# Score steps over four row groups, values begun with the later heads, and a new written order in a two-layer attention and expert kernel

## Chip, core and metric

The kernel runs on one NeuronCore of one Trainium2 chip. The metric is the device time of one execution in microseconds (us). Three runs of the kernel before gave 589.65, 581.01 and 583.12 us; their median is 583.12.

## What is computed

The input is 4 sequences of 512 tokens of width 128, in float32. Two layers follow each other, each of the form x + attention(norm(x)) * silu(experts(norm(x))).

```python
x = L0_attn_x                                   # (4, 512, 128)
xn = _layernorm(x)
s = _L0_attn_ref(xn, ...)                       # 16 heads of 8: compressed + selected + windowed
g = _silu(_L0_ffn_ref(xn, ...))                 # 8 experts, the best 2 of each token
x = x + s * g
xn = _layernorm(x)
s = _L1_attn_ref(xn, ...)                       # 16 heads of 8, full softmax attention, own norm
g = _silu(_L1_ffn_ref(xn, ...))                 # 8 experts, one result kept for each token
x = x + s * g
```

Layer 0's attention adds three softmax attentions weighted by a gate: over 32 compressed blocks of 16 tokens, over the first 8 tokens of the two best blocks, and over a window of 32 tokens. Layer 1's attention is dense over 512 keys.

## The kernel before

The four sequences are called b = 0 to 3. PE is TensorE, DVE VectorE, ACT ScalarE, POOL GpSimd, SP the queue that starts most transfers.

**Layer 0 attention** (`attn0`, L720). Heads lie in four groups of four; a group of four heads is 32 rows of q and k, so one group is one row group of the PE array (`g32`, rows 32g to 32g+31). Windowed scores: for each parity `e` of the 16 blocks of 32 keys and each pair `k` of groups, one step writes 8 blocks x 2 groups of matmuls (L739, 32 rows x 128 columns of weights, 64 columns streamed; each float32 matmul appears as two instructions) into one pair of PSUM banks (`pair`, tag "s", two such pairs exist). The next step is the Exp on ACT (L748), the next the mask product on DVE (L751). Compressed scores (L756, Exp L766, mask L768) go the same way, a pair of groups at a time; selected scores (L780) use two row groups of 64. Then for each half of the tokens two steps of output matmuls (L819, L827, L835) and one step of normalising on DVE (L845 to L866) follow, then transposes, the projection (L880) and its sum.

**Experts** (`experts`, L314). Tokens are sorted by expert through a dispatch (L191) that computes, for tiles of 128 rows, which rows to fetch (`where`, L311) and whose weights to load. Layer 0 has 46 tiles in two dispatches, layer 1 has 23. Four coroutines serve them: `weights` (a 578 KB load from SP, four buffers, L328), `fetches` (an indirect gather from POOL, L339), `hidden` (transposes L354 once for four tiles, their copy L357, then eight matmuls L362 and the relu, L374 on ACT in layer 0 and L376 on DVE in layer 1), and `outputs` (eight matmuls L387, the bias sum L396 on DVE, an indirect scatter from POOL, L399).

**Layer 1 attention** (`attn1`, L1048). There are 64 units: b, four groups `t` of four heads, four blocks `k` of 128 keys. `scores` has three steps for a unit: four matmuls (L1065, one for each head, each in its own row group, two PSUM pairs of tag "s", hp = 0 and 1), then the Exp of hp 0, then that of hp 1 (L1074, 128 x 1024 each). `values` has one step for a unit: eight instructions of L1085 (four heads, each in its own column group of 32, twice for float32) that add into one PSUM bank over four units, and after the fourth a copy out by DVE (L1095). `turned` transposes (L1103), divides (L1109, L1110) and projects (L880).

**The order.** Nothing is scheduled by the compiler: every strand of work is a coroutine named by a character, and `ORDER` (L60) is a string in which each character runs the next step of its strand. Every engine then takes its instructions strictly in that order, and each transfer stands in its queue where it was written. The characters: 0 to 3 norms and logits, 4 to 7 the entry into layer 1, 8 and 9 set-up, a and b the two dispatches of layer 0, c to f values, g to j keys, k to n layer 0's attention, o, p, q, r its weights, fetches, hidden and outputs, s buffers, t and u layer 1's router, v its dispatch, w scores, x values, y to B the turned parts, C, D, E, F layer 1's weights, fetches, hidden and outputs, G to K the end. In layer 1 the old string often reads `wwFwEFECFw`: scores, Exp, an expert's output matmuls, Exp, hidden matmuls of a later tile, the bias sum, its relu, a weight load, a scatter, the next scores.

Written out from that string, with ST for a unit's score matmuls and AV for its values, the old order has units 21 to 24 as: ST22, Exp, AV21, Exp, AV22, ST23, Exp, y of tile 1, Exp, hid of tile 3, ST24.

Of the kernel before, what the change touches and what calls it, by code (L numbers as in the profile page):

```python
# [12 lines left out]
F32 = mybir.dt.float32  # L13
# [3 lines left out]
AF = mybir.ActivationFunctionType  # L17
# [3 lines left out]
P = 128  # L21
B, S, D = 4, 512, 128
# [7 lines left out]
QB = 32  # L30
NJ = S // QB
# [4 lines left out]
SCALE = float(1.0 / np.sqrt(HD))  # L36
# [21 lines left out]


ORDER = """  # L60
v88290282920232032100301301g31g31g3cg1ccg1agggaacggkkaggkkkkkkkkkaakkgkggkkkgaahokpokhohpkaaohap
kpccppcdddkabpphdkhhkqkpqhpqphhkpqhhrkqqkhqkqkhbrklrrlobhqqqhrlolrqrblpqqdpdpidrpleolbrereilqrlo
qrlrlqrelqrlrlqrlqrlrlqrllrqrlpbbbpipllprirlbbbbilliloooiloliqleqlielriqqrmeorrmqrmoqrrqrqorrqrm
pqoiiqmirqrpqprqmomrirmpqrmoqrrqqroqrrqpqrqorrqprqomrrmpqrmoqrrqprqoqrrqpqrqorrqpqromrrmqprqmomr
rmpqrqmoqrrqpqroqrrqprq4mrorm5pqrmoqrrqprqoqrrq4qrqorr44q5qr4oirfp4rfp5fqrqio4j5r4rjpjr5oqrfqrjp
qrm4q4j54mjrjpm4pqqpjrpq4rjjrm5qr55jjrqoq5omjor5rjsqrqfofrrfmq4pq5ppppppppr4oqq4r5rttqtqjqqrmtrr
jmttqrqrrqmrqrrmnrrnnnnonnnonnnonnno44nnnq4q4rnnrrqnqnnrnrrqnqrnrronssoooooqnqr4nrrqnq5n5q5nqwwr
wqrrqqwrw4wrrr4xwwxwxww6wx7wxwy5w5y6x575ww67wx676www6x76ww66wx7wxw6y6wxy7w77w6w76x75ww6w76w67wxu
wxuuww5wwwxv5wxvwwxwxuuuwvwywvxywxwvvwxCCDwCwyDCywxyD6Dww6Dwy6xD6yDwwEyDwxDEyEDxEwDwzEzDwExwwFwE
FEFwwxCwxwwFwE6FECFwwE6DwxE6DwxDw7wzD7x7zwwxwxwwFwEFEFwwxwFxEFEFwwzxzwCwCwxwxwwF7wEFECFwwxw7xw7w  # L70
z7xzwzwwzxzwwwzwxzwwxwFxwFwEFEwExDECwDwxDwxD7ww7wA7xAwxwFwEFECFwwxwxwwFwEFECFwwxwxwxwFwEFECFwwxw
xwwFwEFECFwwExDwEwDwxDDDDDDDDwFEFECFwwFwEFECFAFxAEFECFxwwxwxwwFwEFECFEwEFwEwFECFFEFECFFxFCFEEwwF
wEFECFEFEEFECCCCCFFAFExFEFAxFFEEEwwAxAwAwwxwxwxwAFAwxFFwwAwFAwFwBFFxBwwwBxBwGwwxwxwwBwxBGwGGwxHH
wxGGIIwGGwGwwJJxxxBBBBBBBKK
"""


# [19 lines left out]
class Kernel:  # L97
# [622 lines left out]
    def attn0(self, b, got, gates, pool):  # L720

        nc = self.nc
        a = got[b]
        qT = a["qT"]
        pair = lambda n: self.psum.tile([P, 2, 512], F32, tag="s", name=f"{n}_{b}", bufs=2)
        split = lambda t: t.rearrange("p (k s) -> p k s", s=S)
        pw, pc = [], []
        g32 = lambda g: slice(32 * g, 32 * g + 32)
# [2 lines left out]
        wm = bc(self.cst[:, T_WM : T_WM + 2 * QB], 1, NJ)  # L731
        for e in range(2):
            pw.append(split(self.shared("kx", 2, 4 * S, f"pw{e}_{b}")))
            for k in range(2):
                ps = pair(f"sw{e}{k}")
                for jj in range(NJ // 2):
                    j = 2 * jj + e
                    for g in (2 * k, 2 * k + 1):
                        nc.tensor.matmul(  # L739
                            ps[:, g % 2, jj * 2 * QB : (jj + 1) * 2 * QB],  # L740
                            a["kw"][g32(g), j].rearrange("p h r -> p (h r)"),
                            qT[g32(g), j * QB : (j + 2) * QB],
                            start=True,
                            stop=True,
                        )
                yield
                t = pw[e][:, 2 * k : 2 * k + 2, :]
                nc.scalar.activation(t, ps, AF.Exp, scale=SCALE)  # L748
                yield
                t = t.rearrange("p g (j q) -> p (g j) q", q=2 * QB)  # L750
                nc.vector.tensor_tensor(t, t, wm, ALU.mult)  # L751
                yield
        for k in range(2):
            ps = pair(f"sc{k}")
            for g in (2 * k, 2 * k + 1):
                nc.tensor.matmul(  # L756
                    ps[:, g % 2, :],
                    a["kc"][g32(g)].rearrange("p h n -> p (h n)"),
                    qT[g32(g), 0:S],
                    start=True,  # L760
                    stop=True,
                )
            yield
            t = split(self.shared("p1", 4, 2 * S, f"pc{k}_{b}"))
            pc.append(t)
            nc.scalar.activation(t, ps, AF.Exp, scale=SCALE)  # L766
            yield
            nc.vector.scalar_tensor_tensor(  # L768
                t,
                bc(self.cst[:, T_QI : T_QI + S], 1, 2),  # L770
                self.vec(V_CP),
                t,
                ALU.is_ge,
                ALU.mult,
            )
            yield
        ps = pair("ss")
        for k in range(2):
            r = slice(64 * k, 64 * k + 64)
# [4 lines left out]
                start=True,  # L784
                stop=True,
# [17 lines left out]
        for half in range(2):  # L803
            ps = pair(f"o{half}")
            for i in range(2):
                t = 2 * half + i
# [4 lines left out]
                for g in range(4):  # L811
                    for prev in range(2):
                        for c in range(4):
                            q = 4 * t + c
# [11 lines left out]
                for g in range(4):  # L826
# [4 lines left out]
                        start=True,  # L831
# [216 lines left out]
    def attn1(self, got, pool):  # L1048
# [6 lines left out]
        def scores():  # L1055
            for u in units:
                b, t, k = u
                qs, ks = got[b]
                ps = []
                for hp in range(2):  # L1060
                    n = f"st_{b}_{t}_{k}_{hp}"
                    ps.append(self.psum.tile([P, 2, 512], F32, tag="s", name=n, bufs=2))
                    for i in range(2):
                        r = slice(32 * (2 * hp + i), 32 * (2 * hp + i) + 32)
                        nc.tensor.matmul(  # L1065
                            ps[hp][:, i, :], ks[r, t, k * P : (k + 1) * P], qs[r, t, :],
                            start=True, stop=True,
                        )
                yield
                p[u] = []  # L1070
                for hp in range(2):
                    e = self.shared("p1", 4, 2 * S, f"p1_{b}_{t}_{k}_{hp}")
                    e = e.rearrange("p (i s) -> p i s", i=2)
                    nc.scalar.activation(e, ps[hp], AF.Exp, scale=SCALE)  # L1074
                    p[u].append(e)
                    yield

        def values():
            for u in units:
                b, t, k = u  # L1080
                va, e = self.va[b % 2], p.pop(u)
                if k == 0:
                    av = self.psum.tile([P, 512], F32, tag="av", name=f"av1_{b}_{t}", bufs=1)
                for h in range(4):
                    nc.tensor.matmul(  # L1085
                        av[32 * h : 32 * h + 32, :],
                        va[:, k, (4 * t + h) * 32 : (4 * t + h) * 32 + 32],
                        e[h // 2][:, h % 2, :],
                        start=(k == 0),
                        stop=(k == NT - 1),  # L1090
                    )
                yield
                if k == NT - 1:
                    o[b, t] = self.shared("vk", 2, S, f"oT_{b}_{t}")
                    nc.vector.tensor_copy(o[b, t], av)  # L1095
                    yield
# [1177 lines left out]
```

## Time and profile before

| | us |
|---|---|
| median of three runs | 583.12 |
| lowest and highest | 581.01 and 589.65 |
| the profiled execution, whole | 598.38 |
| its span, first to last instruction | 596.6 |
| mean granted clock of PE in it | 0.863 of full |
| PE busy in it | 495.1 (83%) |
| VectorE busy | 304.5 (51%) |
| ScalarE busy | 236.6 (40%) |
| first score matmul of layer 1 | 354.3 |
| last values matmuls of layer 1 end | 576.9 |

The costliest rows of the groups, with their busy time: L1074 Exp 124.1 us in 128 instructions; L1085 values 91.2 in 512; L387 and L362, the two expert matmuls, 88.2 and 83.4 in 552 each; L739 windowed scores 38.5 in 512; L1065 scores 38.5 in 256; L756 compressed scores 12.8 in 32.

How to read a profile line: in a group or timeline line, L739 is a line of the kernel, then come the engine, the operation, output <- inputs, shapes and "x" how many instructions. PEld is the weight load of a matmul, which is its own instruction. A bracket gives how long the engine was idle before and who released it. Matmuls are pipelined, so the time from one start to the next says more than a single duration. A line of the table by stages gives, after the stretch and its length, the busy time (and count) of PE, PEld, DVE, ACT and POOL, then PE's granted clock, the share of the transfer engines, and GB/s.

### The profile page before, as it was taken

The numbers are of one execution on the slowest core, as the hardware profiler recorded it, in microseconds if no ns is written. First come the engines' busy times: TensorE is split into PE (matmuls) and PEld (weight loads), VectorE is DVE, ScalarE is ACT, GpSimd is POOL, SyncE is SP. The second block draws the span as 40 slices with busy tenths as digits, with TensorE's granted clock in tenths as the row PEclk, the third lists the DMA queues.
The fourth block names the chain that finished last, engine by engine and source line by source line (L and its number), as shares of the span: only waits on it lengthen the run. The fifth ranks groups of instructions, "written<-read, shape, count | busy, mean of one in ns | idle before, by whom it ended". The sixth has DMA issues, their size and how long they took to land.

```text
span 596.6 us, 11079 instructions
## 1 busy us (share of the span) xinstructions
PE 495.1 (83%) x4203; PEld 341.2 (57%) x4203; DVE 304.5 (51%) x843; ACT 236.6 (40%) x401; POOL 188.3 (32%) x194
## 2 busy tenths in 40 slices
PE   1857788896997989788879988788799999999970
PEld 1646467883876977667766772232354445667420
DVE  1686845955263312376955342868234333246263
ACT  0122103342033245423234235665365766643650
POOL 0300412255004357788520132531623031323100
PEclk9975756798569599997976799998899999999995
DMA  7240540276015367893475345422955643554120
GB/s 215 71 89 1 192 91 19 87 192 203 2 30 162 130 206 235 272 247 96 98 238 196 125 149 153 141 72 73 306 167 149 215 134 101 139 197 163 48 86 24
DMA packets 50160, 82.23 MB, mean 138 GB/s; under 512 B 5505, under 2 KB 30225, under 8 KB 50097
## 3 DMA queue, kind: packets, MB, share of 16 engines
q1 hardware_dynamic: 45104, 71.04, 38.0%
q0 software_dynamic: 4416, 9.05, 6.1%
q10 hardware_dynamic: 576, 1.34, 0.6%
q8 instruction: 35, 0.57, 0.4%
q14 instruction: 29, 0.23, 0.1%
HBM read 64.30 MB, written 17.11 MB: 136 GB/s over the span
## 4 chain that ended last, share of the span: by engine, by line
PE 34%; DVE 10%; issue 6%; ACT 4%; DMA 3%; POOL 1%; SPq 0%; ACTq 0%; DVEq 0%; POOLq 0%
PE av L1085 9%; PE y L387 6%; PE hid L362 5%; PE st L1065 4%; ACT p L1074 3%; PE sw L739 1%; DMA xr<-xs,d_where 1%; PE so L880 1%; PE o L827 1%; PE otr L1103 1%; PE o L819 1%; DMA wt<-in_w 1%; POOL xr L339 1%; PE k L1011 1%; PE sc L756 1%
## 5 line engine op out<-in xcount | busy, mean ns | idle before, releaser
L1074 ACT ACTIVATE p<-st 128x1024 f32<-128x1024 f32 x128 | 124.1, 1024 | 87.5 <-PE st L1065 74.9
L399 POOL DMA_INDIRECT ys<-y,d_where x69 | 77.6, 1125 | 234.4 <-DVE y L396 186.0
L387 PE MATMUL y<-wt,h 128*128 128x128 f32 x552 | 88.2, 307 | 23.4 <-ACT h L374 11.6
L339 POOL DMA_INDIRECT xr<-xs,d_where x69 | 71.3, 1034 | 103.1 <-DVE d_where L311 65.2
L1085 PE MATMUL av<-p,va 128*32 128x512 f32 x512 | 91.2, 619 | 11.1 <-ACT p L1074 9.0
L387 PEld LDWEIGHTS y<-wt,h 128*128 128x128 f32 x552 | 75.7, 208 | 40.1 <-ACT h L374 19.6
L374 ACT ACTIVATE h<-hid,wt 128x128 f32<-128x128 f32 x184 | 52.5, 369 | 101.7 <-issue 56.9
L362 PE MATMUL hid<-xts,wt 128*128 128x128 f32 x552 | 83.4, 299 | 1.8 <-ACT h L374 0.6
L362 PEld LDWEIGHTS hid<-xts,wt 128*128 128x128 f32 x552 | 75.3, 211 | 10.3 <-issue 5.9
L396 DVE TENSOR_TENSOR y<-y,wt 128x128 f32<-128x128 f32 x69 | 20.0, 289 | 113.8 <-PE y L387 92.8
L1085 PEld LDWEIGHTS av<-p,va 128*32 128x32 f32 x512 | 14.2, 109 | 52.4 <-ACT p L1074 40.3
L739 PE MATMUL sw<-qT,kw 32*128 32x64 f32 x512 | 38.5, 330 | 3.3 <-ACT kw L616 3.3
L1065 PEld LDWEIGHTS st<-stq,stk 32*128 32x128 f32 x256 | 15.7, 183 | 43.2 <-issue 25.5
L739 PEld LDWEIGHTS sw<-qT,kw 32*128 32x128 f32 x512 | 36.8, 240 | 4.8 <-ACT kw L616 3.4
L1065 PE MATMUL st<-stq,stk 32*128 32x512 f32 x256 | 38.5, 500 | 1.2 <-ACT p L1074 0.8
L376 DVE TENSOR_SCALAR h<-hid,wt 128x128 f32<-128x128 f32 x92 | 25.9, 345 | 15.5 <-PE hid L362 12.4
L819 PE MATMUL o<-v,pw 128*32 128x36 f32 x992 | 19.9, 225 | 12.2 <-issue 12.1
L748 ACT ACTIVATE pw<-sw 128x1024 f32<-128x1024 f32 x16 | 16.4, 1023 | 31.4 <-PE sw L739 26.1
L819 PEld LDWEIGHTS o<-v,pw 128*32 128x32 f32 x992 | 15.6, 132 | 21.4 <-issue 20.6
L751 DVE TENSOR_TENSOR pw<-pw,c_cst 128x1024 f32<-128x1024 f32 x16 | 19.5, 1222 | 10.1 <-ACT pw L748 9.9
L827 PE MATMUL o<-v,pc 128*128 128x36 f32 x128 | 24.2, 346 | 0.0
L827 PEld LDWEIGHTS o<-v,pc 128*128 128x128 f32 x128 | 22.2, 260 | 1.0
(248 smaller groups left out, 599.7 us busy)
## 6 DMA issues: line engine op xcount, KB each, us to landing
wt<-in_w SPq DMA_DIRECT2D x69, 578.0 KB
v<-drv SPq DMA_DIRECT2D x16, 256.0 KB
drq<-hl SPq DMA_DIRECT2D x16, 256.0 KB
stq<-drq SPq DMA_DIRECT2D x4, 1024.0 KB
drk<-hl SPq DMA_DIRECT2D x16, 256.0 KB
stk<-drk SPq DMA_DIRECT2D x4, 1024.0 KB
yg<-ys SPq DMA_DIRECT2D x12, 256.0 KB
xr<-xs,d_where POOLq DMA_INDIRECT x69
```

The lines of the kernel that those rows point to most:

```text
L339: nc.gpsimd.indirect_dma_start(out=rows[i // 4][:, i % 4, :], out_offset=None, in_=self.xs[ks[i // NS]], in_offset=bass.IndirectOffsetOnAx ...
L362: nc.tensor.matmul(ps[:, f, :], wt[:, W_1 + f * P : W_1 + (f + 1) * P], xt[:, i % 4 * P : (i % 4 + 1) * P], start=True, stop=True,)
L374: nc.scalar.activation(h[:, f, :], ps[:, f, :], AF.Relu, bias=b1)
L376: nc.vector.tensor_scalar(h[:, f, :], ps[:, f, :], b1, 0.0, ALU.add, ALU.max)
L387: nc.tensor.matmul(ps[:, 0:D], g["h"][:, f, :], g["w"][:, W_2 + f * D : W_2 + (f + 1) * D], start=(f == 0), stop=(f == NF - 1),)
L399: nc.gpsimd.indirect_dma_start(out=views[i], out_offset=bass.IndirectOffsetOnAxis(ap=to[:, i % NS : i % NS + 1], axis=0), in_=y, in_offset ...
L739: nc.tensor.matmul(ps[:, g % 2, jj * 2 * QB : (jj + 1) * 2 * QB], a["kw"][g32(g), j].rearrange("p h r -> p (h r)"), qT[g32(g), j * QB : (j ...
L819: nc.tensor.matmul(out(2, g, 4, g32(c)), pw[j % 2][:, g, at : at + QB], flat(a["vw"][:, 4 * j + g]), start=(prev == 0), stop=(prev == 1 or ...
L827: nc.tensor.matmul(out(0, g, 4), pc[g // 2][:, g % 2, t * P : (t + 1) * P], flat(a["vc"][:, g]), start=True, stop=True,)
L1065: nc.tensor.matmul(ps[hp][:, i, :], ks[r, t, k * P : (k + 1) * P], qs[r, t, :], start=True, stop=True,)
L1074: nc.scalar.activation(e, ps[hp], AF.Exp, scale=SCALE)
L1085: nc.tensor.matmul(av[32 * h : 32 * h + 32, :], va[:, k, (4 * t + h) * 32 : (4 * t + h) * 32 + 32], e[h // 2][:, h % 2, :], start=(k == 0) ...
```

## The change

It has four parts.

1. In `attn0` one step now writes the windowed scores of all four row groups, in the order 2, 3, 0, 1, into both PSUM pairs; then come two steps of Exp and two of masks. A b has 28 steps where it had 31.
2. The compressed scores are written likewise: one step of matmuls, two of Exp, two of masks.
3. In `attn1` the score matmuls of hp 1 are written before those of hp 0 (the Exps stay in the order 0, 1), and the four heads of the values are taken in the order 2, 3, 0, 1.
4. `ORDER` is another string, of 1263 characters instead of 1275. In layer 0 its first dispatch stands ahead of batch 0's block choice, the first experts ahead of batch 0's output groups, and batch 1's attention is written together after tile 15 of the experts. In layer 1 each unit's score matmuls are written before the values of the unit ahead of it, in all 63 places; the old order has that in 35 of them and the values first in 28. As an example, units 47 to 49: ST48, transposes of four tiles, Exp, AV47, Exp, y of tile 14, copy of values, ST49, hid of tile 16, Exp, AV48, Exp, y of tile 15.

```diff
 ORDER = """
-v88290282920232032100301301g31g31g3cg1ccg1agggaacggkkaggkkkkkkkkkaakkgkggkkkgaahokpokhohpkaaohap
...
+8v839239232083210301321031021g20gg0cg1ccg1agggacagkgagkgkkkkaaaakkkpgppopokkkkopoggpghpkpqkkqhpq
...
 """
...
         for e in range(2):
             pw.append(split(self.shared("kx", 2, 4 * S, f"pw{e}_{b}")))
+            ps = [pair(f"sw{e}{k}") for k in range(2)]
+            for jj in range(NJ // 2):
+                j = 2 * jj + e
+                for g in (2, 3, 0, 1):
+                    nc.tensor.matmul(
+                        ps[g // 2][:, g % 2, jj * 2 * QB : (jj + 1) * 2 * QB],
+                        a["kw"][g32(g), j].rearrange("p h r -> p (h r)"),
+                        qT[g32(g), j * QB : (j + 2) * QB],
+                        start=True,
+                        stop=True,
+                    )
+            yield
             for k in range(2):
-                ps = pair(f"sw{e}{k}")
-                for jj in range(NJ // 2):
-                    j = 2 * jj + e
-                    for g in (2 * k, 2 * k + 1):
-                        nc.tensor.matmul(
...
+                nc.scalar.activation(pw[e][:, 2 * k : 2 * k + 2, :], ps[k], AF.Exp, scale=SCALE)
                 yield
-                t = pw[e][:, 2 * k : 2 * k + 2, :]
-                nc.scalar.activation(t, ps, AF.Exp, scale=SCALE)
-                yield
-                t = t.rearrange("p g (j q) -> p (g j) q", q=2 * QB)
+            for k in range(2):
+                t = pw[e][:, 2 * k : 2 * k + 2, :].rearrange("p g (j q) -> p (g j) q", q=2 * QB)
                 nc.vector.tensor_tensor(t, t, wm, ALU.mult)
                 yield
+        ps = [pair(f"sc{k}") for k in range(2)]
+        for g in (2, 3, 0, 1):
+            nc.tensor.matmul(
+                ps[g // 2][:, g % 2, :],
...
-                ps = []
-                for hp in range(2):
-                    n = f"st_{b}_{t}_{k}_{hp}"
-                    ps.append(self.psum.tile([P, 2, 512], F32, tag="s", name=n, bufs=2))
+                ps = [
+                    self.psum.tile([P, 2, 512], F32, tag="s", name=f"st_{b}_{t}_{k}_{hp}", bufs=2)
+                    for hp in range(2)
+                ]
+                for hp in (1, 0):
                     for i in range(2):
...
-                for h in range(4):
+
+                for h in (2, 3, 0, 1):
                     nc.tensor.matmul(
```

## Prediction before the changed kernel was run

> **What bounds the kernel now.** I read the page first, then the stages, then TensorE's own timeline in the stages that the change touches. The page (busy row, then tenths of each fortieth of the span):
>
> ```profile
> span 596.6 us, 11079 instructions
> PE 495.1 (83%) x4203; PEld 341.2 (57%) x4203; DVE 304.5 (51%) x843; ACT 236.6 (40%) x401; POOL 188.3 (32%) x194
> PEclk9975756798569599997976799998899999999995
> ```
>
> TensorE (PE) is the only engine near full, and its granted clock is often about half in the first two thirds. The stages (columns: busy us of PE, weight loads, DVE, ACT, POOL, then clock and DMA):
>
> ```profile
> 39.00:96.00 57.00, 46.11 (x418) 34.01 (x419) 39.56 (x104) 11.48 (x16) 13.82 (x12) 0.56 0.28 80
> 96.00:175.00 79.00, 69.47 (x748) 58.98 (x747) 46.70 (x116) 22.78 (x54) 20.09 (x16) 0.74 0.32 91
> 310.00:354.00 44.00, 41.54 (x548) 33.21 (x547) 19.97 (x32) 13.17 (x27) 7.76 (x8) 0.80 0.45 160
> 354.00:432.00 78.00, 63.13 (x379) 25.19 (x378) 43.75 (x132) 42.48 (x52) 28.01 (x30) 0.96 0.49 155
> 432.00:512.00 80.00, 78.11 (x542) 38.48 (x542) 28.06 (x80) 53.29 (x56) 17.03 (x19) 1.00 0.46 150
> ```
>
> PE is 80 to 98% busy in all five; from 432 us on it has no hole. So PE's in-order list sets the time, and the question is what of its "busy" is real work. Layer 1's answer is in its timeline:
>
> ```profile
> 434.28 1.97 PE L1085 MATMUL av<-p,va 128*32 128x512 f32 x8 [0.22 <-ACT p L1074]
> 436.18 0.50 PE L1065 MATMUL st<-stq,stk 32*128 32x512 f32 x4
> 436.61 1.16 PE L387 MATMUL y<-wt,h 128*128 128x128 f32 x8
> 437.60 1.06 PE L362 MATMUL hid<-xts,wt 128*128 128x128 f32 x8
> ...
> 439.20 1.07 PE L1085 MATMUL av<-p,va 128*32 128x512 f32 x8
> ```
>
> The same eight values matmuls take 1.97 us when the second Exp is late (heads 0, 1 run, then 2, 3 a second time through the array) and 1.07, about 0.99 to the next start, when both are there. Over the layer L1085 is busy 91.2 us against 64 units x 1.06 = 67.8: some 23 us are the same array time taken twice.
>
> The scores of layer 0 show the other case. Thirty-two windowed matmuls in two row groups take this, and layer 1's four in four row groups take that:
>
> ```profile
> 123.25 2.00 PE L739 MATMUL sw<-qT,kw 32*128 32x64 f32 x32
> 376.20 0.19 PEld L1065 LDWEIGHTS st<-stq,stk 32*128 32x128 f32 x4 [0.84 <-issue]
> ```
>
> That is 60 ns per matmul (1.93 us to the next start), while one weight load of 32x128 lasts 181 to 187 ns; four loads into four row groups end within 0.19 us, so four go side by side.
>
> [...] here 2.65 us of idle before 74.25 is followed by L827 at 1.7 us for eight, where it takes 0.9 elsewhere[...]. [...]
>
> **The change part by part.**
>
> 1. Windowed scores. Sixteen half-steps become eight steps of four row groups. L739 is busy 12.6 us for b=0, 8.0, 9.7 and 8.2 for b=1 to 3. If four groups cost per step what two do now, half goes. For b=1 to 3, where PE is the bound: 25.9/2 = 12.9 us. For b=0 (39 to 54 us) PE then waits for other work; I count 0. Ends: 0 (no overlap gained), 12.9.
>
> 2. Compressed scores. L756 is busy 12.8 us, 4.1 of it b=0's; half of the other 8.7: 4.3 us. Ends 0 and 4.3.
>
> 3. What both add: a step needs both score buffers of PSUM (tag "s", bufs=2), so it waits for two Exps, 1.94 us together, where the old half-step waited for one. It is hidden where expert work (y 0.99, hid 0.99) is written between. For b=2 and 3 it is. For b=1 the new order writes second windows, compressed scores, selected scores and all four output groups with no expert work between: one Exp pair (2.1), one Exp more (1.2) and masks on DVE (about 1.5) stand bare, 5 us. Queued behind on PE are layer 0's tiles from 16 on; their weights (SP) run on meanwhile.
>
> 4. Order of the first 100 us. `where` of route 0 is written at 65.17 because DVE first does batch 0's top-k chain (55.43 to 62.6); the order now puts the dispatch steps first, so fetches, weights (SP) and the first hid (95.53 now) move up by some 15 to 30 us. They pass, on PE, batch 0's output groups and part of b=1's keys; on SP, two weight loads now stand ahead of b=1's value store and wait there for tiles 0 and 1; on POOL nothing else is waiting. PE is idle 10.9 us in 39 to 96; half of that filled is 5 us. With point 3: net 0, ends -8 and +8.
>
> 5. Scores of layer 1. hp=1 first means that PE waits for the later Exp once and all four row groups run together: 0.43 us instead of 0.61 (438.59 to 439.20). The price: score pair 0 no longer runs under Exp 1. Loop: score start to Exp start 0.61, two Exps 1.94, 0.06 to PE: 2.61 us a unit, in which PE needs 0.43 + 0.99.
>
> 6. Values of layer 1, heads 2, 3 first: always 0.99, after Exp 1. That alone gains nothing, since 1.97 from Exp 0 ends when 0.99 from Exp 1 does. The order makes the gain: in the old one, 28 units have their values written ahead of the next scores, so the next scores wait behind the split. That loop shows as 3.58 us (377.88 to 381.46). In the new one all 63 have the scores first, a loop of 2.6. 28 x 0.97 = 27 us at most.
>    Second count: I add for every unit the PE work written up to the next scores (0.43, 0.99, y and hid 0.97, transposes 0.5, projections 0.9) and take 2.6 where it is less. 34 units have more, 111.8 together; 30 are filled up to 2.6: 78. Sum 190 us. From the first scores (354.3) to the last values (576.9) it takes 222.6 now. The fetch wait around 422 to 427 (some 4 us) and DVE's copies remain, say 8 more: 198. I take 25. Ends 8 and 32.
>
> 7. From the last values to the end, 20 us: transposes, projection, certificate. Unchanged.
>
> Sum: 12.9 + 4.3 + 0 + 25 = 42 us. The profiled execution took 598.4; it would take 556. The median of the runs is 583.1, 15.3 less, and that execution has half clock in it (0.56 to 0.80 in layer 0's rows). At full clock points 1 and 2 are smaller: 12 half-steps x 1.93/2 = 11.6 and 6 x 1.06/2 = 3.2. So 40, of which I take 38 off the median: **545 us**.
>
> **Rivals.**
> - A, the two-row scores are bound by something that four groups share (loads of 128 columns, issue). For it: L739's loads are busy 36.8 us of its 38.5. Against it: the four loads in 0.19 us, and L819's 64 matmuls in 0.7. Then only layer 1 gains: 583 - 25 + 3 (the coarser steps of point 3, unpaid) = 561.
> - B, the coarser handoff eats the gain: both score pairs wait for the later Exp, ACT idles 0.67 a unit, and holes appear where I counted none. Layer 1 gains 8 and b=1 loses 5: 583 - 8 - 15 + 5 = 565.
> - C, slower: the clock. In the 30 light units PE works 1.42 of 2.6 us (55%), where the split kept it at 67%. If that lets the clock fall to half, a light unit takes 3.03 but one with an expert tile 6.6 instead of 3.3. It decides from about 13 such units (13 x 3.3 = 43 us) on; with 15: 583 - 38 + 49 = 594. Against it: a third of the work lies between, and 363 to 384 us at 67% stayed at full clock.
> - D, the clock helps: earlier experts and denser scores keep layer 0 at full clock. Its half-clock stretches from 96 to 345 us sum to about 88 us (twice what the clock lacks of 1 in the rows: 79 x 0.52, 135 x 0.22 for 175 to 310 us at 0.89, 44 x 0.40) and cost about 40; half of that gone: 525.
>
> **How the numbers follow.** Forecast (534 to 556) 0.50, D 0.16, A 0.10, B 0.16, C 0.08. About 2% is what a measurement of this kernel can tell from no change, so faster means below 571: forecast, D, nine tenths of A and eight tenths of B give 0.50 + 0.16 + 0.09 + 0.13 = 0.88; same 0.05; slower 0.07. Eight in ten: C lies outside above and a part of D below, so 520 to 570.
>
> **What would show it.** Right: L739's busy time falls from 38.5 to about 20 and its 64 matmuls take about 2 us at full clock; L1085 falls from 91 to about 68 with no piece of 1.97; light units repeat every 2.6 us; first hid before 80 us; first scores of layer 1 at 325 to 340, last values some 195 to 205 later. Wrong: 64 windowed matmuls in 3.9 us (A), ACT idle ahead of L1074 larger than 87.5 us with the loop over 3 us (B), hid and y at 1.9 us each after 354 us (C).

## The result, and the profile after

The changed kernel takes 581.2 us (median of 20 runs, 573.6 to 593.3), the kernel before beside it 587.3 us (20 runs, 581.0 to 594.2). The ratio is 0.985, with a 95% interval of 0.981 to 0.989: 1.5% faster, where 545 us had been forecast. All ratios here leave out executions over 1.5% above the fastest of the same kernel (the medians of all 20 give 0.990), and where too few are left, medians stand alone. On another chip the same two kernels gave 0.978 (0.971 to 0.984). Chips differ more than that: the kernel before took 588 us on some of those used here and 555 on others, so kernels are compared by their ratio to the kernel before on the same chip.

The profile that the forecast was made from took 598 us. A second profile of the kernel before took 587.1 us (experiment e1_before) and is the one compared with from here on. The profiled execution of the changed kernel took 576.9 us.

The page's groups that the forecast spoke of, changed kernel (busy time, mean ns | idle time before, what ended most of it):

```profile
L1076 ACT ACTIVATE p<-st 128x1024 f32<-128x1024 f32 x128 | 124.1, 1022 | 84.6 <-PE st L1067 75.6
L1088 PE MATMUL av<-p,va 128*32 128x512 f32 x512 | 76.1, 669 | 0.7 <-DVE y L396 0.5
L1067 PE MATMUL st<-stq,stk 32*128 32x512 f32 x256 | 43.7, 525 | 9.3 <-ACT p L1076 8.1
L738 PE MATMUL sw<-qT,kw 32*128 32x64 f32 x512 | 23.8, 316 | 6.5 <-ACT kw L616 3.3
```

And the same groups in the second profile of the kernel before:

```profile
L1074 ACT ACTIVATE p<-st 128x1024 f32<-128x1024 f32 x128 | 124.0, 1024 | 87.1 <-PE st L1065 77.4
L1085 PE MATMUL av<-p,va 128*32 128x512 f32 x512 | 92.0, 619 | 10.8 <-ACT p L1074 9.4
L1065 PE MATMUL st<-stq,stk 32*128 32x512 f32 x256 | 38.5, 500 | 1.2 <-ACT p L1074 0.8
L739 PE MATMUL sw<-qT,kw 32*128 32x64 f32 x512 | 39.3, 335 | 3.3 <-ACT kw L616 3.3
```

PE's work did shrink: windowed scores 39.3 to 23.8, values 92.0 to 76.1 us. But layer 1's scores grew from 38.5 to 43.7 and wait 9.3 instead of 1.2, and ACT's Exps of layer 1 stand idle as long as before. One step of 64 windowed matmuls, from PE's timeline of the changed kernel:

```profile
290.94 2.01 PE L738 MATMUL sw<-qT,kw 32*128 32x64 f32 x64
```

That is twice the matmuls in the 2.00 us that 32 took before: here the four row groups run side by side.

Where the time went is seen when the span is cut at three events: layer 1's first scores, layer 1's first expert tile (first hid), the last values. The columns are the stretch and its length, busy time (instructions) of PE, weight loads, DVE, ACT, POOL, then granted clock, DMA share, GB/s. Kernel before, second profile:

```profile
0.00:345.40 345.40, 284.11 (x2824) 235.02 (x2824) 193.26 (x534) 104.22 (x252) 128.43 (x130) 0.84 0.48 141
345.40:420.50 75.10, 62.21 (x363) 23.52 (x362) 42.46 (x128) 42.27 (x52) 26.27 (x28) 0.95 0.48 151
420.50:565.60 145.10, 140.40 (x1003) 75.05 (x1003) 59.69 (x170) 89.51 (x97) 34.88 (x36) 1.00 0.47 147
565.60:585.30 19.70, 4.12 (x22) 2.66 (x18) 8.24 (x13) 0.00 (x0) 0.00 (x0) 0.62 0.11 32
```

Changed kernel:

```profile
0.00:333.50 333.50, 265.13 (x2824) 222.26 (x2824) 195.86 (x534) 103.86 (x255) 126.25 (x130) 0.84 0.51 147
333.50:413.10 79.60, 64.83 (x396) 26.89 (x395) 43.70 (x130) 47.74 (x55) 26.07 (x28) 0.85 0.45 139
413.10:553.60 140.50, 131.70 (x963) 72.59 (x967) 58.32 (x166) 83.82 (x91) 35.22 (x37) 0.95 0.49 154
553.60:575.00 21.40, 5.97 (x26) 3.71 (x18) 8.58 (x14) 0.00 (x0) 0.00 (x0) 0.50 0.10 29
```

Read it by rows. Layer 0 is 11.9 us shorter, for 19.0 us less PE work. Layer 1, rows two and three, takes 220.2 us before and 220.1 after: its first part is 4.5 us longer, its second 4.6 shorter. The tail is 1.7 longer. Layer 1's forecast gain of 25 us isn't there at all. In the third row PE is 94 to 97% busy, and eight hid matmuls of the changed kernel take 2.01 us at a clock of 0.50 (at 181.54 us) and 1.06 at 1.00 (at 525.83). So there the clock should count: it fell from 1.00 to 0.95, and 0.05 of 140.5 us is 7 us of full-speed work (an estimate from these lines). A part of what the new order gains may be lost in that; no run separates it.

### The profile page after: what moved, and what is told of

Read it like the earlier page. It is cut to its first block, busy times and chain, and to the rows that moved or that the text cites. A ratio compares the mean times of both kernels' runs of the same rounds, so it can differ in the third digit from the quotient of the medians.

```text
span 575.0 us, 10989 instructions
## 1 busy us (share of the span) xinstructions
PE 467.6 (81%) x4203; PEld 325.5 (57%) x4203; DVE 306.5 (53%) x843; ACT 235.4 (41%) x401; POOL 187.5 (33%) x194
## 5 line engine op out<-in xcount | busy, mean ns | idle before, releaser
L1076 ACT ACTIVATE p<-st 128x1024 f32<-128x1024 f32 x128 | 124.1, 1022 | 84.6 <-PE st L1067 75.6
L399 POOL DMA_INDIRECT ys<-y,d_where x69 | 72.5, 1051 | 213.2 <-DVE y L396 188.8
L1088 PE MATMUL av<-p,va 128*32 128x512 f32 x512 | 76.1, 669 | 0.7 <-DVE y L396 0.5
L1067 PE MATMUL st<-stq,stk 32*128 32x512 f32 x256 | 43.7, 525 | 9.3 <-ACT p L1076 8.1
L738 PE MATMUL sw<-qT,kw 32*128 32x64 f32 x512 | 23.8, 316 | 6.5 <-ACT kw L616 3.3
L747 ACT ACTIVATE pw<-sw 128x1024 f32<-128x1024 f32 x16 | 15.8, 1024 | 31.5 <-PE sw L738 14.8
L738 PEld LDWEIGHTS sw<-qT,kw 32*128 32x128 f32 x512 | 21.3, 226 | 8.7 <-issue 4.4
L1098 DVE COPY oT<-av 128x512 f32<-128x512 f32 x16 | 11.0, 690 | 25.6 <-PE av L1088 20.9
L828 PE MATMUL o<-v,pc 128*128 128x36 f32 x128 | 21.7, 319 | 0.9 <-issue 0.9
L828 PEld LDWEIGHTS o<-v,pc 128*128 128x128 f32 x128 | 19.9, 234 | 1.8 <-issue 0.8
L1088 PEld LDWEIGHTS av<-p,va 128*32 128x32 f32 x512 | 10.5, 113 | 17.9 <-issue 14.9
L820 PE MATMUL o<-v,pw 128*32 128x36 f32 x992 | 16.6, 220 | 3.3 <-issue 3.3
```

The costliest lines, as they stand in the source:

```text
L399: nc.gpsimd.indirect_dma_start(out=views[i], out_offset=bass.IndirectOffsetOnAxis(ap=to[:, i % NS : i % NS + 1], axis=0), in_=y, in_offset ...
L738: nc.tensor.matmul(ps[g // 2][:, g % 2, jj * 2 * QB : (jj + 1) * 2 * QB], a["kw"][g32(g), j].rearrange("p h r -> p (h r)"), qT[g32(g), j * ...
L828: nc.tensor.matmul(out(0, g, 4), pc[g // 2][:, g % 2, t * P : (t + 1) * P], flat(a["vc"][:, g]), start=True, stop=True,)
L1067: nc.tensor.matmul(ps[hp][:, i, :], ks[r, t, k * P : (k + 1) * P], qs[r, t, :], start=True, stop=True,)
L1088: nc.tensor.matmul(av[32 * h : 32 * h + 32, :], va[:, k, (4 * t + h) * 32 : (4 * t + h) * 32 + 32], e[h // 2][:, h % 2, :], start=(k == 0) ...
```

## The experiments

Ratios are to the kernel before on the same chip, with their 95% intervals. The theory that was formed from the profiles ("theory 1" below): layer 0's row groups are a real gain, partly given back; in layer 1 what the split of the values cost is now waited for by the scores, so the new order gains nothing. Rivals: layer 1's edits themselves cost what the order gains; the granted clock falls and eats the gain (it averaged 0.881 over 27 runs of the kernel before on one chip, and 0.846 over the 20 of the changed kernel; side by side on e4's chip 0.917 and 0.879).

**e1_before.** No edit.

> The kernel before, unchanged, profiled once more: the profile shown so far took 598.4 us, 15 above the median of its runs. All theories expect about 583 to 590 us, and the same order of work. It tells which of the 21.6 us between the two profiles belong to the change: a stage that is shorter here too than in the first profile of before does not count.

587.1 us. Layer 0 took 345.4 us where the first profile had 354.3; layer 1 took 220.2 where that had 222.0. So 9 of the first profile's excess were layer 0's alone, and the comparison above is between usual executions.

**e1_four_rows: layer 0's row groups alone.** In the kernel before's steps (abridged):

```diff
-            for k in range(2):
-                ps = pair(f"sw{e}{k}")
-                for jj ...: for g in (2 * k, 2 * k + 1): matmul(ps ...)
-                yield
+            ps = [pair(f"sw{e}{k}") for k in range(2)]
+            for jj ...: for g in (2, 3, 0, 1): matmul(ps[g // 2] ...)
+            for k in range(2):
+                yield
```

and the same for sc.

> Kernel before with one edit, its written order kept character for character: each windowed and compressed score step of layer 0 writes all four row groups where its first half stood, and the second half's step writes nothing. Theory 1 (the row groups' gain is real, and what layer 0 saves is largely given back in waits and lower clock): L739's 64 matmuls in about 2 us at full clock, 15 us less PE work, and the time 3 to 8 us lower. Theory 2 (the gain of layer 0 is whole, and the new written order or layer 1 loses it again): 12 to 16 us lower. If the double buffer itself is the loss: no change or slower.

0.985 (0.980 to 0.991), 581.0 against 587.6 us. The row falls from 39.3 to 25.4 us busy; layer 1's first scores come at 339.1 instead of 345.4. That is 6.6 us by the medians and 8.8 by the ratio, about theory 1's 3 to 8; the whole gain of 12 to 16 isn't there. This one edit, under the old order, gains as much as the whole change.

**e1_two_rows: the opposite edit in the changed kernel.** Its step writes the matmuls pair by pair:

```diff
-            for jj in range(NJ // 2):
-                for g in (2, 3, 0, 1):
+            for k, jj in [(k, jj) for k in range(2) for jj in range(NJ // 2)]:
+                for g in (2 * k, 2 * k + 1):
```

> Changed kernel with one edit: within its windowed score step the 64 matmuls are written pair by pair, so that only two row groups are side by side, as before; buffers, steps and order stay those of the changed kernel. The row goes from 24 back to about 38 us busy (64 in 3.9 us at full clock) in all theories. Theory 1 (the new order has layer 0 behind other waits in part): 4 to 9 us slower than the changed kernel. Forecast's point 1 (PE is the bound for the batches 1 to 3): 12 us slower. If layer 0 is bound by other work altogether: 0 to 2.

1.001 (0.998 to 1.004): the row is back at 37.9 us busy and the whole gain of the change is gone. From 0.985 to 1.001 is 9 to 10 us. By these ratios the row groups were worth some 9 us in both orders, and everything else in the change came to nothing.

**e1_layer1_edits: layer 1's edits under the old order.** `for hp in (1, 0)` in the scores, `for h in (2, 3, 0, 1)` in the values.

> Kernel before with layer 1's two edits alone (score pair 1 written first, heads 2 and 3 first in the values), its written order kept. Theory 1 (the split of the values was a wait for the second Exp, not work of the array): the values' row falls from 91 to about 68 us busy, the score row's or values' idle time rises by as much, and the time stays within 3 us. Theory of the forecast: the edits alone gain nothing either, the order gains; so 0. Theory 2 (score pair 1 first costs the overlap of one score pair with the other Exp): up to 10 us slower, ACT idle ahead of layer 1's Exp up by 5 to 15 us.

1.021 (1.017 to 1.025): 12 us slower, beyond theory 1's 3 us and what theory 2 named. Its groups, values first:

```profile
L1086 PE MATMUL av<-p,va 128*32 128x512 f32 x512 | 74.9, 659 | 34.1 <-ACT p L1075 32.0
...
L1075 ACT ACTIVATE p<-st 128x1024 f32<-128x1024 f32 x128 | 124.2, 1023 | 99.3 <-PE st L1066 88.8
```

The values are busy 17.1 us less than in the kernel before (92.0) and idle 23.3 us more (10.8): the split had been a wait for the second Exp that looked like work. Without it the kernel is not faster but slower, and the first pair's values, which had run under the second Exp, no longer do. ACT's idle grew by 12.2 us, as much as the loss. Which of the two edits does it was not tried in the old order.

**e2_values_later: the order's part of point 6 alone.** As above, and in the written order the 28 values steps that stood ahead of the next unit's scores go right behind them; nothing else is moved.

> Kernel before with layer 1's two edits, and in its written order only one thing moved: the 28 values steps of layer 1 that stand ahead of the next unit's scores go right behind them. This is the forecast's point 6 alone. Forecast: 25 us below the kernel before, so about 562. Theory 1 (a values step moved behind the scores saves the wait for the second Exp, but with pair 1 first the scores wait for that same Exp, so a tile unit and a light unit still take 6.0 us together): 0 to 6 us below the kernel before, and some 12 to 18 below the two edits with the old order.

1.009 (1.004 to 1.014). The move wins back 7 of the 12 us and never gets below the kernel before. Values, ACT, scores:

```profile
L1075 ACT ACTIVATE p<-st 128x1024 f32<-128x1024 f32 x128 | 124.1, 1022 | 87.7 <-PE st L1066 82.9
...
L1086 PE MATMUL av<-p,va 128*32 128x512 f32 x512 | 76.3, 671 | 2.7 <-ACT p L1075 1.4
...
L1066 PE MATMUL st<-stq,stk 32*128 32x512 f32 x256 | 49.0, 525 | 12.3 <-ACT p L1075 11.5
```

The wait is gone from the values (34.1 to 2.7) and stands before the scores (1.4 to 12.3, and 49.0 busy instead of 42.0, since pairs that arrive apart take longer: 0.50 us each, as all four together, in the last section). ACT's idle is 87.7, where the kernel before has 87.1. Layer 1 took 228.8 us in its profile, at a clock of 0.78 and 0.97 in its two stretches, where the kernel before had 0.95 and 1.00, so some of the loss may be the clock's; but the forecast's 562 us is refuted by its own mechanism, done alone.

**e2_four_rows_values_later.** The four row groups and the same 28 moves, with score pair 0 and heads 0 to 3 first as before.

> Kernel before with four row groups in layer 0's scores (its steps kept) and the same 28 values steps moved behind the next scores, but score pair 0 first and heads 0 to 3 as before. Theory 1: light units at about 2.0 us, no split of the values, so the 8.7 us of the four row groups and 5 to 12 more: about 570, and faster than the changed kernel. Theory 2 (layer 1 is set by PE's work and the chain to its experts): 578 to 582, no gain over the four row groups alone. Forecast's point 6 with layer 0's gain: 555.

0.986 (0.981 to 0.991), the same as the four row groups alone: theory 2, and a miss of theory 1, which had 5 to 12 us more. Moving the values is worth nothing with pair 0 first either. There too the wait came up before the scores (idle 10.7 us and busy 45.0, where e1_four_rows has 1.2 and 38.5); ACT's idle fell from 87.0 to 77.6, and the time didn't follow.

**e2_hp01, e2_layer1_back, e3_heads_only: layer 1's two edits undone in the changed kernel**, the first alone, both, the second alone.

```diff
-                for hp in (1, 0):
+                for hp in range(2):
...
-                for h in (2, 3, 0, 1):
+                for h in range(4):
```

> Changed kernel with one edit: layer 1's score pair 0 is written before pair 1 again; values stay with heads 2 and 3 first, order unchanged. Theory 1 (pair 1 first makes every light unit wait for the later Exp: 2.6 us a unit; with pair 0 first its two matmuls run under the second Exp and a light unit takes about 2.0): 4 to 9 us faster than the changed kernel, ACT's idle ahead of layer 1's Exp down by 5 to 15 us; not more, since the first layer-1 expert tile waits for a chain that the units don't set. Theory 2 (layer 1 is bound by PE's work and the chain to the experts, the loop matters little): within 2 us. Forecast's point 5 taken by itself (four groups together save 0.18 us a unit): 5 us slower.

> Changed kernel with both edits of layer 1 undone (score pair 0 first, values in heads 0 to 3), the new written order kept. All values already stand behind the next scores, so both Exps should be past when they begin. Theory 1: the same as with the scores' edit alone undone, within 2 us, and faster than the changed kernel by 4 to 9; the values' row at 68 to 80 us busy without pieces of 1.97. Theory 2 (heads 2 and 3 first matter in the new order): 5 us or more slower than with only the scores' edit undone.

> Changed kernel with one edit: the values of layer 1 in heads 0 to 3 again; score pair 1 stays first, order unchanged. It completes the square of the two edits of layer 1 in the new order. Theory 1 (all values stand behind the next scores, both Exps are past, so the order of heads costs nothing): within 2 us of the changed kernel; the difference of some 6 us between the two kernels with pair 0 first is then the spread of the granted clock. Theory 2 (heads 2 and 3 first cost something of their own): 5 to 8 us faster than the changed kernel.

Ratios 0.979 (0.974 to 0.984), 0.969 (0.964 to 0.973) and 0.984 (0.980 to 0.989). With pair 1 first, undoing the heads' order does nothing, as theory 1 said. With pair 0 first the kernel was faster than the changed kernel's 0.985, by 0.6 and 1.6%, though ACT's idle did not fall by the 5 to 15 us of theory 1 (84.7 in e2_hp01, 84.6 in the changed kernel). The 0.979 and 0.969 differ in the heads' order alone, and theory 1 had put these two within 2 us: a miss, unless it is the spread of six runs each (566.7 to 594.2 us). The three ran on two chips and not beside the changed kernel, so the changed kernel and the one with both edits undone were run again side by side (e4, below).

**e3_warm: work added to keep the clock up.** In 16 of the first 22 units, four values matmuls on columns of zeros ahead of the real ones (abridged):

```diff
+                if k > 0 and units.index(u) < 22:
+                    for h in range(4):
+                        matmul(av[32 * h : 32 * h + 16, :], va[:, k, c + 16 : c + 32],
+                               e[h // 2][:, h % 2, :], start=False, stop=False)
```

> Changed kernel with work added and nothing else: in 16 of the first 22 units of layer 1 the four values matmuls are preceded by four more on columns of zeros (they add zero), 0.99 us of PE each time, 16 us in all. Theory clock (PE works 1.42 of 2.6 us in the light units, and that lets the clock fall to half from 352 to 380 us, as it doesn't in the kernel before): the half-clock time there, 24 us, shrinks to under 12, the mean clock rises by 0.01 to 0.02, and the kernel is no slower or 2 to 6 us faster although PE does more. Theory stall (the clock falls because PE waits 8.7 us in unit 9, whatever the loop does): the half-clock time stays at 20 to 28 and the time rises by 0 to 4. If PE's work is the bound there: 16 us slower.

0.982 (0.977 to 0.986), 545.7 us, beside 546.1 for e3_heads_only on the same chip, which serves as the changed kernel there. Their stretch from the first scores to layer 1's first tile, e3_heads_only and then e3_warm:

```profile
313.50:392.10 78.60, 63.93 (x395) 25.99 (x394) 43.63 (x130) 47.91 (x56) 24.78 (x27) 0.85 0.42 138
```

```profile
309.50:390.10 80.60, 70.80 (x524) 28.39 (x523) 43.74 (x130) 47.95 (x56) 24.81 (x27) 0.94 0.43 134
```

The clock went from 0.85 to 0.94 (over the whole kernel and six runs, from 0.879 to 0.891), so here more work in the light units went with a higher clock, and the stretch got no shorter. But the added work takes PE's time itself: 70.8 us busy instead of 63.9. Sixteen us more of work cost 2 us here, so PE isn't the only bound of this stretch; how long it would be at 0.94 without that work isn't shown.

**e3_shift: the order around unit 9.** All steps from unit 9 to 40 that are neither scores nor values, except batch 1's entry and the end of batch 2's, stand three units later.

> Changed kernel, all instructions the same, another written order in layer 1 alone: from unit 9 to 40 the steps that are neither scores nor values stand three units later, so that three light units fill the wait of unit 9 (12.6 us from its scores to the next for 3.8 us of work) and the units 41 to 43 are no longer empty; batch 1's entry and the last steps of batch 2's stay. Theory 1 (the stall and the clock that falls in it are what the new order loses in layer 1): 4 to 9 us faster than the changed kernel, less half-clock time between 350 and 385 us, the first layer-1 expert tile not later. Theory 2 (the chain to the experts sets everything up to its tile, and the 23 tiles and the units behind it are short of room for nothing): within 2 us. Rival: the steps moved are the chain itself, each three units late: up to 8 us slower.

0.985 (0.980 to 0.990): no gain. The same stretch of its profile:

```profile
310.90:399.90 89.00, 71.19 (x432) 27.30 (x431) 44.09 (x131) 53.67 (x61) 26.46 (x28) 0.86 0.46 146
```

It became 10.4 us longer (89.0 against 78.6) with three units more in it, and the stretch to the last values 1.8 shorter (130.0 against 131.8). The rival named in the expectation is what happened: the steps moved are the chain itself.

**e3_shift_back**: the same order with both edits of layer 1 undone.

> The same shifted order with both edits of layer 1 undone (score pair 0 first, heads 0 to 3): a candidate for a version faster than both kernels. Theory 1: the two gains add, 560 to 568 us. Theory 2: 570 to 574, as with the edits undone alone.

546.4 us against 554.8 for the kernel before, no interval: no better than e3_heads_only. A miss of theory 1.

**e4_layer0_new and e4_layer1_new: each half of the change alone.** The written orders and the code were joined at layer 1's first scores: new up to there and old behind, and the reverse. Two more ran on the same chip: the changed kernel (e4_after) and it with layer 1's edits undone (e4_layer1_back).

> One half of the change: the new code and the new written order up to layer 1's first scores, then layer 1's code and order of the kernel before. From the stages: 333.5 us to the first scores, then 220.2 and 19.7 as in the kernel before: 1.5 to 2.5% below the kernel before, as much as the whole change. Theory forecast (13 us of layer 0 and 25 of layer 1): also 2%. Rival (the halves need each other, because layer 0's new order leaves steps where layer 1's old order doesn't look for them): under 1%.

> The other half: code and order of the kernel before up to layer 1's first scores, then layer 1's new code and new order. Own theory (units that were split are now units that wait, the two orders have the same sum of 185 us when a unit costs at least 2.6): 345 + 220 + 21, within 1% of the kernel before. Forecast's point 6: 25 us, 4% below the kernel before. Rival (light units at a lower clock): 1 to 2% slower.

> The changed kernel again, as the yardstick on this chip: 1.5% below the kernel before, as measured; 0.5 to 2.5% with another chip's clock.

> The changed kernel with layer 1's two edits undone, again, now beside the changed kernel. If pair 0 under the second Exp is worth its 4 to 5 us after the first expert tile: 0.6 to 1.8% below the changed kernel. If the earlier difference was the clock of single executions: within 0.5%.

The kernel before took 554.1 us on this chip. New layer 0: 552.2 (no interval), 0.4% less. New layer 1: 0.993 (0.990 to 0.995), 4 us less. Changed kernel: 0.978 (0.971 to 0.984). With layer 1's edits undone: 0.985 (0.979 to 0.991), the same median as the changed kernel (544.7 and 544.8). So layer 1's half is worth 4 us, not 25; and layer 0's half, expected at 1.5 to 2.5%, was worth 2 us on this chip when done alone. The whole change takes 9 us off the median, more than its halves together: behind the new layer 1, layer 0's half makes 551.1 into 544.8, which is 6 us. The rival of the first expectation, that the halves need each other, fits this; with so few runs it isn't settled. The layer-0 rows of e4_layer1_new (old layer 0) and e4_layer0_new (new):

```profile
0.00:314.40 314.40, 260.91 (x2836) 215.69 (x2836) 193.98 (x535) 105.35 (x256) 128.51 (x130) 0.90 0.54 157
```

```profile
0.00:312.60 312.60, 251.60 (x2836) 212.15 (x2837) 194.51 (x534) 104.95 (x256) 125.73 (x130) 0.87 0.56 159
```

PE is busy 9.3 us less and the stage ends 1.8 us earlier: 7.5 us turned into idle time. In e4_layer1_back, which has the new layer 0 too, it is 11.9 us less and 4.5 us earlier. The clock of this stage is lower in the new one (0.87 against 0.90).

**e5_spread and e5_spread_back: batch 1's packed attention opened.** The written order puts the expert tiles 16 to 19 between the steps of batch 1's attention instead of behind it, with their weights fetched earlier; the second has layer 1's edits undone as well.

> Changed kernel, all instructions the same, another written order in one stretch of layer 0: the expert tiles 16 to 19, which stand behind batch 1's attention, stand between its steps (behind the second windowed scores, the compressed scores, the selected scores, and between the output groups), and their weights' fetches as early as their buffers allow. Theory packing (layer 0's saving was lost in batch 1's bare waits, at half clock and with the weights held up): the half-clock time from 140 to 185 us falls from 34 to under 20, layer 1's first scores come 5 to 10 us earlier, and the kernel is 4 to 10 us faster than the changed kernel (2.3 to 3.5% below the kernel before). Theory weights (from batch 1 on layer 0 is bound by fetches of weights and rows that follow one another anyway): 0 to 2 us. Rival: the tiles' own waits for rows and weights now stand in front of batch 1's attention: slower by up to 5.

> The same spread order, with layer 1's two edits undone: the candidate for the fastest version. Where the two edits cost nothing and give nothing, as side by side on the last chip: within 0.5% of the spread order alone. Where pair 0 under the second Exp is worth something: up to 1% faster.

The stretch from 140 to 184 us, changed kernel and then e5_spread:

```profile
140.00:184.00 44.00, 35.90 (x493) 30.15 (x491) 25.30 (x53) 12.29 (x22) 8.31 (x8) 0.62 0.30 84
```

```profile
140.00:184.00 44.00, 37.13 (x588) 32.05 (x586) 26.50 (x58) 18.57 (x44) 17.24 (x15) 0.96 0.60 157
```

The clock came back (0.62 to 0.96), 95 more matmuls fit, data moved at 157 instead of 84 GB/s, and tile 16 began at 156.9 instead of 181.5 us. But by tile 36 the lead was 4 us (274.6 and 278.5), layer 1's first scores came at 330.9 instead of 333.5, and the time is 0.989 (0.983 to 0.995): no gain over 0.985. The theory that this packing alone swallowed layer 0's saving has fallen. The clock, though, came back only in this stretch; over all of layer 0 it is 0.85, where the changed kernel has 0.84:

```profile
0.00:330.90 330.90, 264.06 (x2824) 221.93 (x2824) 195.64 (x534) 104.24 (x255) 128.75 (x130) 0.85 0.53 148
```

e5_spread_back gave 0.972 (0.962 to 0.981), 1.7% below e5_spread on the same chip (0.9% by the medians).

## Why the prediction was wrong

Four of the 36 us between forecast and result lie in the starting value: 583.1 was the median of three runs, and 20 gave 587.3. Of the signs named, the windowed row (23.8 us busy), the values' row (76.1), the light units (2.59 us), the first hid (66.0) and layer 1's first scores (333.5) came about as forecast. The last values did not: they ended 220 us after the first scores, not 195 to 205.

**Points 1 and 2 (row groups): mechanism right, size too large.** 64 matmuls take 2.01 us and the row lost 15.5 us. In time the row groups were worth 9 us, where 14.8 had been counted at full clock; layer 0's half of the change was worth 2 to 6 us on another chip. The assumption that failed is that PE is the bound of batches 1 to 3 everywhere: 7.1 of 19.0 us in one profile, and 7.5 of 9.3 in another, became waits. What sets the time there instead stays open.

**Points 3 and 4 (batch 1's bare waits, earlier experts): net 0 was right, by another way.** The waits are there: 4.26 us ahead of the compressed scores and 1.12 ahead of the selected ones, at a clock of 0.56 and 0.50. The first hid came at 66.0 us (forecast: before 80). But the lead melts: counted from 0, tile 15 begins at 143.0 instead of 199.9 us, tile 27 at 232.1 instead of 240.4. e5_spread put tiles between these steps and moved layer 0's end by no more than 2.6 us. An earlier tile is worth something only if the work behind it also moves up.

**Point 5 (pair 1 first): the loop was right, the reason for it wrong.** Two light units of the changed kernel in its timeline, ACT and PE:

```profile
342.19 1.07 PE L1088 MATMUL av<-p,va 128*32 128x512 f32 x8
342.36 1.94 ACT L1076 ACTIVATE p<-st 128x1024 f32<-128x1024 f32 x2 [0.66 <-PE st L1067]
343.44 0.50 PE L1067 MATMUL st<-stq,stk 32*128 32x512 f32 x2 [0.19 <-ACT p L1076]
344.35 0.50 PE L1067 MATMUL st<-stq,stk 32*128 32x512 f32 x2 [0.41 <-ACT p L1076]
...
344.95 1.94 ACT L1076 ACTIVATE p<-st 128x1024 f32<-128x1024 f32 x2 [0.66 <-PE st L1067]
```

342.36 to 344.95 is 2.59 us, the 2.61 of the forecast. But the four groups don't run together: the pairs start 0.91 us apart, the first right after Exp 0, the second right after Exp 1. It fits a buffer that goes to the tile written first as soon as it is free: pair 1, written first, starts with the slot that Exp 0 frees. Pair 0, which the next Exp 0 needs, gets the later one, and ACT stands idle for 0.66 us a unit. Writing the pairs in the other order doesn't bring them together, it only chooses which of them is early; with pair 0 first, in e2_layer1_back, they start 0.91 us apart too.

**Point 6 (values behind the scores, 25 us): this is the step that failed.** Both counts did. The first took each split's 0.97 us off the time. In the old order a unit with its values ahead took 3.58 us and the tile unit beside it 2.4, 5.99 together. In the new one the light unit takes 2.59 and a tile unit 3.41 (0.43 + 0.99 + 1.94 = 3.36 of scores, values, y and hid), 6.00 together. The split was the wait for the second Exp; the scores wait for that Exp now. e2_values_later shows it: the wait left the values' row and came up in the scores' row.

The second count, 190 us plus 8 of waits against 222.6 measured, compared a sum with a measurement. The same sum made for the old written order (work up to the next scores, at least 2.6 us) gives 186 us, and for the new one 185. The count says that the orders are equal (the prediction had 190 for the new one). In the first pair of profiles they were, 220.2 and 220.1; on e4's chip the old order took 217.8 us (e4_layer0_new) and the new one 213.5, 212.0 and 210.0, a gain of 4 to 8. The difference between 190 and 222 was not the split but what the sum leaves out, and this is as large in the new order: between unit 9's scores and unit 10's lie 12.57 us for 3.8 us of work, since PE's list has layer norm transposes there whose inputs arrive 2.78 and 1.83 us late.

What sets the first 75 to 80 us of layer 1 was not worked out by the forecast at all: the way from layer 0's last tiles through layer norm, router and fetches to the first expert tile. It was 75.1 us before and 79.6 after; neither added work with a higher clock nor other places for the light units shortened it.

**Point 7 (tail):** 19.7 to 21.4 us, at a clock of 0.50 instead of 0.62. Nothing was tried on it, but e1_layer1_edits, in the old order, shows the same 21.5 us at 0.50, so layer 1's edits rather than the order seem to bring it.

**The rivals.** A is refuted by the 2.01 us. B had the right place and the wrong sign to look for: its layer-1 gain of 8 was nearer to the 0 to 4 found, but ACT's idle fell to 84.6 and the loop isn't over 3 us. C's sign appeared in part: the clock fell, from 0.99 ahead of 355.31 to 0.50 behind it, though from 345 to 355 us no wait of PE is longer than 0.82 us. That light units, busy for 55% of their time, let the clock fall was the forecast's estimate. The waits here are 0.18 to 0.82 us; in the kernel before longer ones, of 1.17, left the clock at 1.00 (last section), so these runs don't settle what brings it down. C's price came out wrong: it supposed some 15 units with an expert tile at half clock, and behind the first tile the clock was 0.95. D didn't come: layer 0's clock is 0.84 before and after. In two stretches the clock was brought back (0.85 to 0.94 in e3_warm, 0.62 to 0.96 in e5_spread) and neither kernel became measurably faster; but one paid with added work, and in the other the half clock stood elsewhere in the layer (0.85 over all of it). So the rival that the lower clock eats a part of the gain isn't refuted.

**What stays open.** Which chain ends layer 0 when PE has 7 us less to do isn't settled: it isn't batch 1's packing alone, and the clock isn't excluded, since over the whole layer it stayed as low. Nor is it known whether layer 0's and layer 1's halves need each other. Whether pair 0 first is better in the new order differs between the runs (0.9 to 1.7% in e5, 0 in e4), and the reason wasn't found. The changed kernel with both edits undone is the fastest version seen (0.969 on one chip), though on another it only equals the changed kernel.

## What to carry to other kernels

A count that prices the new order must first be made on the old one: if it doesn't give the measured time there, its difference to that time is not a gain. A piece of "busy" time that appears only when an input is late may be a wait: here the values' busy time fell from 92.0 to 74.9 us in e1_layer1_edits and their idle time rose from 10.8 to 34.1. And it may only move to the next user of the same input: in e2_values_later the idle time fell to 2.7 us ahead of the values and rose from 1.4 to 12.3 ahead of the scores. What a stretch at a lower clock costs the whole kernel was not shown. Work added to one in e3_warm went with a clock of 0.94 instead of 0.85, but PE was busy 6.9 us longer, so that test tells whether the filling pays, not what the clock alone is worth.

## What was not expected of the hardware

- The clock fell to half without a long wait: in the changed kernel it was 0.50 from 355.31 to 376 us, and in the 10 us ahead of that PE was busy 7.72 us and waited at most 0.82 at a time. Yet in the first profile of the kernel before, several units with waits of 1.17 us, at about the same busy share (which counts the split's waits as work), ran at a clock of 1.00. The two stretches, changed kernel first:

```profile
345.31:355.31 10.00, 7.72 (x52) 2.24 (x44) 6.43 (x11) 7.97 (x10) 2.07 (x2) 0.99 0.87 273
```

```profile
363.00:384.00 21.00, 15.76 (x84) 3.77 (x81) 13.03 (x40) 12.20 (x15) 6.47 (x6) 1.00 0.64 200
```

- The score pairs that arrive apart take 0.50 us each (changed kernel, 343.44 and 344.35) where all four together take 0.50 in all (347.25): layer 1's scores are busy 38.5 us in the kernel before and 49.0 in e2_values_later, with the same 256 matmuls.
- The same kernel takes 555 us on some chips and 588 on others, and the granted clock differs with it: 0.919 on average over 11 runs there, 0.881 over 27 on one of the others.
